# A graph layer on one Trainium2 core: comparison nodes moved to PSUM, edge statistics in groups of four banks, one spill store placed earlier

## The chip, the cores and the metric

The kernel runs on one core of a Trainium2 chip. The metric is the device time in microseconds (us) of that core; lower is better. Five engines work side by side, each with its own queue of instructions: TensorE (PE in the profile, its weight loads PEld), VectorE (DVE), ScalarE (ACT), GpSimd (POOL) and SyncE (SP). Transfers are issued by SP, ACT and POOL and carried out by 16 DMA engines.

## The reference

```python
def _mlp(h, W, b, gamma, beta):
    h = relu(h @ W + b)
    mu = mean(h, axis=0); var = mean(square(h - mu), axis=0)
    return gamma * (h - mu) * rsqrt(var + EPS) + beta
node_feat = _mlp(x, W_node, ...)                 # x: 12500 x 96
edge_feat = _mlp(edge_attr, W_edge, ...)         # 412500 x 4 -> 96
message   = _mlp(concat([x[row], x[col], edge_feat]), W_msg, ...)
agg       = segment_sum(message, col, 12500)
out       = layernorm(x + agg + node_feat)
```

Here `row` is the edge's source and `col` its target. The edges are sorted by target. Each of the three networks normalizes over all of its rows, so the statistics over all 412,500 edges have to be complete before a message can be made.

## The kernel before, in words

**Units.** Edges are worked on in tiles of 128, four tiles to a *group* of 512 (`GT`, `GE`), four groups to a *block* (`BG`). There are 806 groups and 202 blocks. Because the edges are sorted, a group's targets lie in a window of 31 nodes (`WN`), and the four windows of a block start 16 nodes apart (`WS`).

**Tables.** The source part of the message is a table lookup: `table` (L140) multiplies all nodes by a third of the message weights and writes `p_tab` and `q_tab` to memory. Rows of `p_tab` are fetched for every edge by `gather` (L158): one indirect DMA on POOL (L162) for each tile of 128 edges, 3223 in all. The first 48 of them take raw rows of `x` instead, before the table exists.

**Gathering ahead.** The first 26 blocks are gathered while the earlier stages run: `blocks` (L167) is a generator. Each `next(store)` issues 16 gathers on POOL into one of two `stage` buffers, and then a store of the block to a `spill` area in memory on SP's queue (L173). The order of SP and POOL is written out by hand here, so the places of the calls of `next(store)` (L182, L335, L336, L344, L349) are the places of stores in SP's queue, among the other transfers. Blocks 0 and 1 go with the first table, 2 to 5 with the second, 6 to 8 with the node stage (at its steps 0, 4 and 10), the other 17 with the edge stage. After them come the first 25 groups (100 gathers) of a ring of 25 group buffers, `pg` (L353).

**Node stage.** `nodes` (L241): 25 products of 512 nodes (L248), relu on ACT (L249), statistics on DVE (L250), normalization in place (L256, L257), then 98 products that transpose and center (L262), evacuated on DVE (L266) and stored as `y0_d` by SP (L269). SP's queue has `places` (L221) ahead of that.

**Edge stage.** `edge_norm` (L273) computes the edge network for its statistics alone. 606 products of 128 x 512 (L290: three for each block, on packed rows) are each written into one PSUM bank of a two-bank buffer `pr`, four buffers. After two products ACT takes both through relu into SBUF (`r`, L294, four buffers) and DVE runs one `bn_stats` for each (L296). The inputs `ea` are loaded by SP in chunks of eight blocks, 24 products each (L284), into two buffers. SP's queue holds these loads and the spill stores in one order: a load that waits for a buffer keeps the store behind it back, and a store that waits for its gathers keeps the load behind it back.

**Message stage.** `fast` (L365 on) works through `steps`, one for each group, in an order written out by hand for all five engines (L499). The blocks gathered on the fly ("late", 176) and the spilled ones ("early", 26, read back by L408) are mixed, about seven late to one early. For a group: `linear` (L443) makes four products z (128 x 96) in one of two PSUM buffers; `message` (L451) adds the gathered rows, `hs` = z + `pg` (L463, DVE), and every second group ACT writes relu of `hs` into `h` (L465). `sums` (L471) multiplies each tile of `h` by itself (L480), which yields both the sums by target and the Gram matrix for the statistics. For a block: `edges` (L433) makes four products into the four banks of one `pr` buffer; `prepare` turns them into the next block's `left` operand, relu on ACT (L440) and a comparison on DVE (L441); `add` takes the sums of the block out of PSUM (L493, L494). At the first group of a block, DVE also writes the rows that say which edge belongs to which node of its window (L457): `h` = (`rel` == `iota`), 128 x 496 elements. `rel` (the target's place in the block) and `iota` (the nodes' numbers, 4 x 31) both lie in SBUF.

DVE's order around a block's start is: `hs` of the last group of the block before, L457, `hs` of group 0, of group 1, of group 2, L441, L493 twice, L494. PE's order is: z of group 0, sums, z of group 1, sums, the four products of `edges`, z of group 2, sums, z of group 3, sums. A ring buffer becomes free when its group's `hs` is done; then POOL issues the four gathers of the group 25 places ahead (L528). For an early block no ring buffer is freed.

**Finish.** L704 to L734: the normalized sums are added to `y0`, the layer norm is applied and the result stored.

Of the kernel before, what the change touches and what calls it, by code (L numbers as in the profile page):

```python
# [11 lines left out]
F32 = mybir.dt.float32  # L12
I32 = mybir.dt.int32
AF = mybir.ActivationFunctionType
OP = mybir.AluOpType
AX = mybir.AxisListType
ET = mybir.EngineType
PSUM = bass.MemoryType.PSUM
DRAM = bass.MemoryType.DRAM

N, C, E, ED = 12500, 96, 412500, 4
EPS = 1e-5
P = 128
# [3 lines left out]
GT, GE, BG = 4, 512, 4  # L27
NT = -(-E // P)
NG = -(-NT // GT)
NBL = -(-NG // BG)  # L30
NTP, NGP = NBL * BG * GT, NBL * BG
EP = NGP * GE
EK = ED + 1
Q = 32
NS = 3
# [12 lines left out]
WN, WS, WM = 31, 16, 7  # L48
# [6 lines left out]
SKEW = 6  # L55
HB, RB = 2, 3
CL, CE = 2, 2
J = 8


# [12 lines left out]
def gnn(ctx, tc, t):  # L73
    nc = tc.nc
# [26 lines left out]
    iota = const.tile([P, BG, WN], F32, name="iota")  # L101
# [4 lines left out]
    wide = const.tile([P, P], F32, name="wide")  # L106
# [70 lines left out]
    store = blocks()  # L177
# [12 lines left out]
    for i in range(NS):  # L190
        k, n = Q * i, C - Q * i
# [81 lines left out]
    def edge_norm():  # L273

        with tc.tile_pool(name="es", bufs=2) as work, tc.tile_pool(name="es1", bufs=1) as one, \
                tc.tile_pool(name="es_ps", bufs=4, space=PSUM) as ps:
            stats = one.tile([P, NS, NBL, 6], F32, name="estats")
            for b in range(NBL):
                if b % J == 0:
                    yield  # L280
                    ea = work.tile([P, J, GE], F32, name="ea")
                    n = min(J, NBL - b)
                    for i in range(NS):
                        nc.sync.dma_start(ea[Q * i:Q * i + 2 * EK, :n, :],  # L284
                                          t["ea"][EK * i:EK * (i + 2), b:b + n, :])
                for i in range(NS):
                    k = NS * b + i
                    if k % 2 == 0:
                        pr = ps.tile([P, 2, GE], F32, name="pr")
                    nc.tensor.matmul(pr[:, k % 2, :], wide[Q * i:Q * i + 2 * EK, :],  # L290
                                     ea[Q * i:Q * i + 2 * EK, b % J, :], start=True, stop=True)
                    if k % 2:
                        r = work.tile([P, 2, GE], F32, name="r", bufs=4)
                        nc.scalar.activation(r, pr, AF.Relu)  # L294
                        for o in (1, 0):
                            nc.vector.bn_stats(stats[:, (k - o) % NS, (k - o) // NS, :], r[:, 1 - o, :])  # L296

            part = one.tile([P, NS, 2], F32, name="part")
            square = one.tile([P, NS], F32, name="square")
            for i in range(NS):  # L300
                nc.vector.bn_aggr(part[:, i, :], stats[:, i, :, :].rearrange("p a b -> p (a b)"))
            nc.vector.tensor_mul(square, part[:, :, 0], part[:, :, 0])
            nc.vector.tensor_add(part[:, :, 1], part[:, :, 1], square)
            pick = one.tile([P, NS, C], F32, name="pick")
            nc.vector.memset(pick, 0.0)
            for i in range(NS):
                for o in range(-P * i % C - C, P, C):
                    lo, hi = max(o, 0), min(o + C, P)
                    if lo < hi:
                        to = pick[:, i, lo - o:hi - o]  # L310
                        nc.vector.tensor_add(to, to, ident[:, lo:hi])
            pm = ps.tile([C, 2], F32, name="pr")
            for i in range(NS):
                nc.tensor.matmul(pm, pick[:, i, :], part[:, i, :], start=i == 0, stop=i == NS - 1)
            aggr = one.tile([C, 2], F32, name="eaggr")
            nc.vector.tensor_scalar(aggr, pm, float(NBL * GE) / E, None, op0=OP.mult)
            sq = one.tile([C, 1], F32, name="sq")
            nc.vector.tensor_mul(sq, aggr[:, 0:1], aggr[:, 0:1])
            nc.vector.tensor_sub(sq, aggr[:, 1:2], sq)
            nc.vector.tensor_scalar(aggr[:, 1:2], sq, 0.0, None, op0=OP.max)  # L320
            a_e, c_e = norm(aggr, v["g_edge"], v["beta_edge"], "edge")
            pb = ps.tile([1, C], F32, name="pr")
            nc.tensor.matmul(pb, c_e, w_msg[:, 2, :], start=True, stop=True)
            nc.vector.tensor_add(bias, pb, b_msg)
            nc.vector.tensor_scalar(w_e, w_msg[:, 2, :], a_e, None, op0=OP.mult)

    def fast(ring):
# [3 lines left out]
        with tc.manual_schedule(engines={ET.SP, ET.Pool}):  # L331
            with tc.tile_pool(name="tab_w", bufs=1) as work, tc.tile_pool(name="tab_ps", bufs=2, space=PSUM) as ps:
                for i, _ in enumerate(table(q_tab[WM:WM + NN, :], w_msg[:, 1, :], work, ps, (nc.sync,), 8)):
                    if i in (0, 2, 5):
                        next(store)  # L335
            next(store)  # L336
            nc.sync.dma_start(q_tab[:WM, :], zero[:WM])
            for r in range(WM + NN, WT, 64):
                n = min(64, WT - r)
                nc.sync.dma_start(q_tab[r:r + n, :], zero[:n])  # L340
            places()
            for i, _ in enumerate(nodes()):
                if i in (0, 4, 10):
                    next(store)  # L344
            xpool.close()
            n = 0
            for i, _ in enumerate(edge_norm()):
                if 73 * i >= 50 + 100 * n:
                    next(store, None)  # L349
                    n += 1  # L350
            for _ in store:
                pass
            got = {g: ahead_of(g) for g in range(SPILL, SPILL + RING)}  # L353
# [11 lines left out]
        with tc.tile_pool(name="fix", bufs=1) as fix, tc.tile_pool(name="msg", bufs=2) as work, \  # L365
# [11 lines left out]
            hb = [fix.tile([P, BG, GT, P], F32, name=f"h{i}") for i in range(HB)]  # L377
            for x in hb:
                nc.vector.memset(x[:, :, :, C:C + 1], 1.0)

            eas, block, prs, zs, pas, pair = {}, {}, {}, {}, {}, [None]

# [60 lines left out]
            def linear(k):  # L443
                s, g = steps[k]
                n = min(GT, NT - g * GT)
                zs[k] = ps.tile([P, GT, C], F32, name="z")
                for i in range(n):
                    nc.tensor.matmul(zs[k][:, i, :], left[s % 2][:KR, g % BG, i * P:(i + 1) * P],  # L448
                                     rhs[:KR, s % RB, g % BG, :], start=True, stop=True)

            def message(k):  # L451
                s, g = steps[k]
                n = min(GT, NT - g * GT)
                i = g % BG
                h, z, pg = hb[s % HB], zs.pop(k), got.pop(g)
                if i == 0:
                    nc.vector.tensor_tensor(  # L457
                        h[:, :, :, C + 1:C + 1 + WN], rel[:, g:g + BG, :].unsqueeze(3).to_broadcast([P, BG, GT, WN]),
                        iota.unsqueeze(2).to_broadcast([P, BG, GT, WN]), op=OP.is_equal)
                if i % 2 == 0:  # L460
                    pair[0] = work.tile([P, 2, GT, C], F32, name="hs")
                hs = pair[0]
# [35 lines left out]
            n, ahead = len(steps), SPILL + RING  # L498
# [270 lines left out]
```

## Time and profile before

| what | value |
|---|---|
| median of three runs | 5365.72 us (5353.82 to 5367.68) |
| the profiled execution's own time | 5379.39 us |
| its span in the profile | 5377.6 us |
| granted TensorE clock, mean | 0.665 |
| tables and node stage | 0 to 304 us |
| edge stage (L284 to the last L296) | 304 to 1006 us |
| message stage (first to last L463) | 1045 to 5314 us |
| finish | 5323 to 5378 us |

The page of a profile gives, engine by engine, the busy time and its share of the span, then the costliest groups of instructions: line, engine, operation, output and inputs, shapes, how many, total busy time, mean time of one in ns, and the idle time of the engine just before them with what ended it. A timeline row gives the start, the duration, the engine and line, and in brackets the idle time before and who ended it; "remote" and "issue" mean that the profile names no instruction as the releaser. A windows row gives, for a stretch of time, each engine's busy us (and the number of instructions), then TensorE's clock, the share of the DMA engines and GB/s. Ends of matmuls are modelled: when PE's products really are complete is seen better from the start of the instruction that waits for them.

### The profile page before, as it was taken

What the parts mean: (1) busy time and instruction counts of PE and PEld (TensorE: products, weight loads), DVE (VectorE), ACT (ScalarE), POOL (GpSimd) and SP (SyncE); (2) the same over time, 40 slices, a digit from 0 to 9 for tenths busy, and PEclk for the clock granted to TensorE, in tenths of its full rate; (3) what the DMA queues carried; (4) which work ended last, traced back from release to release, by engine and by line L of the source; (5) the groups of instructions that cost most, each with busy time, mean ns of one, the idle gap of its engine ahead of it and who ended that gap; (6) DMA issues with size and microseconds to landing.
All of it is one profiled execution on the core that took longest, in us unless ns stands there. A gap on an engine that the chain in (4) does not pass through costs nothing. (4 is left out here: it accounts for less than half of the span.)

```text
span 5377.6 us, 46715 instructions
## 1 busy us (share of the span) xinstructions
PE 3364.1 (63%) x16705; PEld 2570.3 (48%) x16705; DVE 1699.3 (32%) x2622; ACT 1077.6 (20%) x1015; POOL 3106.6 (58%) x3244
## 2 busy tenths in 40 slices
PE   5566662666656666665667666656666666666668
PEld 5333330354545545544445554544455545545447
DVE  1445551622222322222222322322232222223225
ACT  0224441411111111111111111111111111111112
POOL 5454456155566656666666666666666666666661
PEclk9755555566666766667676766666766666666667
DMA  5332332111111111111111111111111111111112
GB/s 165 112 97 61 71 68 48 29 33 37 39 44 38 43 42 44 43 38 42 42 43 45 42 38 43 44 42 45 37 43 42 41 45 36 43 43 42 44 37 84
DMA packets 188578, 270.80 MB, mean 50 GB/s; under 512 B 121095, under 2 KB 121480, under 8 KB 187330
## 3 DMA queue, kind: packets, MB, share of 16 engines
q0 software_dynamic: 103136, 158.62, 12.2%
q1 hardware_dynamic: 77120, 98.40, 6.6%
q10 hardware_dynamic: 8080, 10.71, 0.7%
q8 instruction: 133, 2.18, 0.2%
q14 instruction: 109, 0.89, 0.1%
HBM read 225.90 MB, written 41.60 MB: 50 GB/s over the span
## 5 line engine op out<-in xcount | busy, mean ns | idle before, releaser
L162 POOL DMA_INDIRECT pg<-p_tab,src x2807 | 2690.8, 959 | 1767.1 <-DVE hs L463 922.8
L448 PE MATMUL z<-rhs,left 128*128 128x96 f32 x6446 | 1222.7, 339 | 878.3 <-issue 672.8
L448 PEld LDWEIGHTS z<-rhs,left 128*128 128x128 f32 x6446 | 1093.2, 249 | 1183.6 <-issue 903.1
L480 PE MATMUL pa<-h 128*97 128x128 f32 x6446 | 1246.3, 331 | 556.2 <-issue 551.6
L480 PEld LDWEIGHTS pa<-h 128*97 128x97 f32 x6446 | 1015.4, 209 | 654.7 <-issue 653.3
L463 DVE TENSOR_TENSOR hs<-z,pg 128x384 f32<-128x384 f32 x702 | 385.2, 555 | 2599.2 <-remote 1537.6
L465 ACT ACTIVATE h<-hs 128x768 f32<-128x768 f32 x402 | 338.9, 843 | 2867.6 <-DVE hs L463 1846.0
L290 PE MATMUL pr<-ea,wide 10*128 10x512 f32 x1212 | 405.4, 1074 | 285.7 <-issue 177.6
L162 POOL DMA_INDIRECT stage<-p_tab,src x368 | 351.0, 954 | 369.6 <-DMA spill<-stage 240.0
L440 ACT ACTIVATE left<-pr 96x2048 f32<-96x2048 f32 x202 | 377.2, 1867 | 643.6 <-remote 439.7
L441 DVE TENSOR_SCALAR left<-pr 31x2048 f32<-31x2048 f32 x202 | 462.9, 2291 | 108.3 <-ACT left L440 75.5
L296 DVE BATCH_NORM_STATS2 estats<-r 128x6 f32<-128x512 f32 x606 | 365.8, 678 | 326.8 <-issue 191.1
L433 PE MATMUL pr<-ea,we 6*127 6x512 f32 x1404 | 411.1, 808 | 62.6 <-issue 47.5
L290 PEld LDWEIGHTS pr<-ea,wide 10*128 10x128 f32 x1212 | 209.6, 320 | 480.2 <-issue 291.8
L294 ACT ACTIVATE r<-pr 128x1024 f32<-128x1024 f32 x303 | 297.1, 1024 | 458.0 <-remote 290.0
L433 PEld LDWEIGHTS pr<-ea,we 6*127 6x127 f32 x1404 | 117.9, 223 | 206.6 <-issue 190.6
L457 DVE TENSOR_TENSOR h<-rel,iota 128x496 f32<-128x496 f32 x202 | 134.6, 666 | 0.0
L463 DVE TENSOR_TENSOR hs<-z,pb 128x384 f32<-128x384 f32 x104 | 56.6, 554 | 233.1 <-remote 85.2
L150 PE MATMUL pt<-w_msg,xp 96*128 96x96 f32 x392 | 88.7, 421 | 60.4 <-issue 37.1
L493 DVE TENSOR_TENSOR agg<-pa,agg 97x62 f32 x404 | 90.1, 223 | 85.4 <-remote 54.8
L150 PEld LDWEIGHTS pt<-w_msg,xp 96*128 96x128 f32 x392 | 85.5, 330 | 63.4 <-issue 48.6
L494 DVE TENSOR_TENSOR gram<-pa,gram 97x388 f32<-97x388 f32 x202 | 111.4, 551 | 0.1
(107 smaller groups left out, 634.7 us busy)
## 6 DMA issues: line engine op xcount, KB each, us to landing
pg<-p_tab,src POOLq DMA_INDIRECT x2807
spill<-stage SPq DMA_DIRECT2D x26, 768.0 KB
pb<-spill SPq DMA_DIRECT2D x26, 768.0 KB
ea<-in_ea SPq DMA_DIRECT2D x75, 160.0 KB
rhs<-q_tab SPq DMA_DIRECT2D x202, 46.5 KB
ea<-in_ea SPq DMA_DIRECT2D x352, 20.0 KB
stage<-p_tab,src POOLq DMA_INDIRECT x368
q_tab<-trow SPq DMA_DIRECT2D x7, 672.0 KB
```

The lines of the kernel that those rows point to most:

```text
L150: nc.tensor.matmul(pt[:, g, :], xp[:, k:k + P], w, start=True, stop=True)
L162: nc.gpsimd.indirect_dma_start(out=pg[:, i, :], out_offset=None, in_=tab[:, :], in_offset=bass.IndirectOffsetOnAxis(ap=idx[:, k:k + 1], ax ...
L290: nc.tensor.matmul(pr[:, k % 2, :], wide[Q * i:Q * i + 2 * EK, :], ea[Q * i:Q * i + 2 * EK, b % J, :], start=True, stop=True)
L294: nc.scalar.activation(r, pr, AF.Relu)
L296: nc.vector.bn_stats(stats[:, (k - o) % NS, (k - o) // NS, :], r[:, 1 - o, :])
L433: nc.tensor.matmul(prs[s][:C + WN, i, :], we[Q * i:Q * i + EK + 1, :], block[s][Q * i:Q * i + EK + 1, :], start=True, stop=True)
L440: nc.scalar.activation(x[:C, :n, :], pr[:C, :n, :], AF.Relu)
L441: nc.vector.tensor_scalar(x[C:C + WN, :n, :], pr[C:C + WN, :n, :], 0.0, None, op0=OP.is_equal)
L448: nc.tensor.matmul(zs[k][:, i, :], left[s % 2][:KR, g % BG, i * P:(i + 1) * P], rhs[:KR, s % RB, g % BG, :], start=True, stop=True)
L463: nc.vector.tensor_add(hs[:, i % 2, :n, :], z[:, :n, :], pg[:, :n, :])
L465: nc.scalar.activation(h[:, i - 1:i + 1, :, :C], hs, AF.Relu)
L480: nc.tensor.matmul(pas[s][:, g % BG, :C + 1 + WN], h[:r, i, :C + 1], h[:r, i, :C + 1 + WN], start=i == 0, stop=i == n - 1)
```

## The change

Three edits. The nodes' numbers that the comparison at a block's start reads are copied once to the unused columns 384 to 507 of one of the two PSUM banks of z, which are now allocated by hand, and the comparison reads them there. Since reader and writer share a bank, the built program has the comparison (L466 there) wait for TensorE's z of group 0, which it did not do before; `hs` of group 0 stands behind it, as before. The edge statistics go through PSUM and ScalarE four products at a time instead of two; `pr` has two buffers of four banks instead of four of two, `r` three buffers of four instead of four of two. And one `next(store)` is added ahead of the node stage, behind `places`; the edge stage then has one block less to gather and store, the last. The number of instructions on PE, POOL and SP stays as it was; ACT has 151 fewer relus in the edge stage, and DVE one copy more.

```diff
+BANKS = 4
...
     def edge_norm():
-                tc.tile_pool(name="es_ps", bufs=4, space=PSUM) as ps:
+                tc.tile_pool(name="es_ps", bufs=2, space=PSUM) as ps:
...
                     k = NS * b + i
-                    if k % 2 == 0:
-                        pr = ps.tile([P, 2, GE], F32, name="pr")
-                    nc.tensor.matmul(pr[:, k % 2, :], wide[Q * i:Q * i + 2 * EK, :],
+                    if k % BANKS == 0:
+                        pr = ps.tile([P, BANKS, GE], F32, name="pr")
+                    nc.tensor.matmul(pr[:, k % BANKS, :], wide[Q * i:Q * i + 2 * EK, :],
                                      ea[Q * i:Q * i + 2 * EK, b % J, :], start=True, stop=True)
-                    if k % 2:
-                        r = work.tile([P, 2, GE], F32, name="r", bufs=4)
-                        nc.scalar.activation(r, pr, AF.Relu)
-                        for o in (1, 0):
-                            nc.vector.bn_stats(stats[:, (k - o) % NS, (k - o) // NS, :], r[:, 1 - o, :])
+                    if k % BANKS == BANKS - 1 or k == NS * NBL - 1:
+                        r = work.tile([P, BANKS, GE], F32, name="r", bufs=3)
+                        n = k % BANKS + 1
+                        nc.scalar.activation(r[:, :n, :], pr[:, :n, :], AF.Relu)
+                        for o in range(n):
+                            j = k - n + 1 + o
+                            nc.vector.bn_stats(stats[:, j % NS, j // NS, :], r[:, o, :])
...
             places()
+            next(store)
             for i, _ in enumerate(nodes()):
                 if i in (0, 4, 10):
                     next(store)
...
+            zb = [ps.tile([P, GE], F32, name=f"z{i}", bufs=1) for i in range(2)]
+            nodes_of = zb[0][:, GT * C:GT * C + BG * WN].rearrange("p (k w) -> p k w", w=WN)
+            nc.vector.tensor_copy(nodes_of, iota)
...
             def linear(k):
-                zs[k] = ps.tile([P, GT, C], F32, name="z")
+                zs[k] = zb[k % 2][:, :GT * C].rearrange("p (t c) -> p t c", c=C)
...
                     nc.vector.tensor_tensor(
                         h[:, :, :, C + 1:C + 1 + WN], rel[:, g:g + BG, :].unsqueeze(3).to_broadcast([P, BG, GT, WN]),
-                        iota.unsqueeze(2).to_broadcast([P, BG, GT, WN]), op=OP.is_equal)
+                        nodes_of.unsqueeze(2).to_broadcast([P, BG, GT, WN]), op=OP.is_equal)
```

## The prediction, made before the changed kernel ran

> **What bounds the kernel now.** I read the page first: busy shares, then the costliest groups.
>
> ```profile
> PE 3364.1 (63%) x16705; PEld 2570.3 (48%) x16705; DVE 1699.3 (32%) x2622; ACT 1077.6 (20%) x1015; POOL 3106.6 (58%) x3244
> ...
> L162 POOL DMA_INDIRECT pg<-p_tab,src x2807 | 2690.8, 959 | 1767.1 <-DVE hs L463 922.8
> ...
> L463 DVE TENSOR_TENSOR hs<-z,pg 128x384 f32<-128x384 f32 x702 | 385.2, 555 | 2599.2 <-remote 1537.6
> ...
> L296 DVE BATCH_NORM_STATS2 estats<-r 128x6 f32<-128x512 f32 x606 | 365.8, 678 | 326.8 <-issue 191.1
> ...
> L294 ACT ACTIVATE r<-pr 128x1024 f32<-128x1024 f32 x303 | 297.1, 1024 | 458.0 <-remote 290.0
> ...
> L457 DVE TENSOR_TENSOR h<-rel,iota 128x496 f32<-128x496 f32 x202 | 134.6, 666 | 0.0
> ```
>
> No engine is full, and PE and POOL wait for each other through `hs`. The windows view says what ends last. Here are two blocks of the message stage (the first without gathers, near the end; the second with) and two stretches of the edge stage (with and without); the columns after the length are busy us of PE, PEld, DVE, ACT, POOL, then TensorE's clock.
>
> ```profile
> 5263.63:5272.85 9.22, 8.47 (x74) 7.38 (x74) 5.84 (x9) 3.56 (x3) 0.00 (x0) 1.00 0.02 7
> 2517.40:2539.70 22.30, 12.70 (x72) 10.57 (x72) 5.94 (x10) 3.56 (x3) 14.42 (x16) 0.73 0.14 35
> ```
>
> ```profile
> 840.00:860.00 20.00, 3.70 (x8) 1.01 (x8) 2.57 (x4) 2.05 (x2) 15.13 (x16) 0.50 0.23 50
> 940.00:960.00 20.00, 20.00 (x75) 11.99 (x72) 20.00 (x35) 16.66 (x18) 0.00 (x0) 0.50 0.30 63
> ```
>
> The same block takes 9.2 us without gathers and 22.3 us with 16 of them; in the edge stage PE makes four products in 20 us under gathers and some 37 without. So PE crawls while POOL gathers, and after an uninterrupted *train* of gathers it stands almost still: the timeline of the edge stage has relus of two products 10.5 to 11.2 us apart from 802 to 913 us, against 0.9 to 1.6 us outside. Why, the trace does not name; that it holds is enough. The timeline of the block above shows how the message stage turns:
>
> ```profile
> 2514.12 0.95 POOL L162 DMA_INDIRECT pg<-p_tab,src  x1 [3.28 <-DVE hs L463]
> ...
> 2517.87 0.95 POOL L162 DMA_INDIRECT pg<-p_tab,src  x1 [0.30 <-issue]
> 2518.30 0.55 DVE L463 TENSOR_TENSOR hs<-z,pg 128x384 f32<-128x384 f32 x1
> 2518.77 0.67 DVE L457 TENSOR_TENSOR h<-rel,iota 128x496 f32<-128x496 f32 x1
> ...
> 2519.12 1.13 POOL L162 DMA_INDIRECT pg<-p_tab,src  x1 [0.30 <-issue]
> 2519.53 0.56 DVE L463 TENSOR_TENSOR hs<-z,pg 128x384 f32<-128x384 f32 x1
> 2520.56 0.95 POOL L162 DMA_INDIRECT pg<-p_tab,src  x1 [0.30 <-issue]
> ...
> 2536.80 0.56 DVE L463 TENSOR_TENSOR hs<-z,pg 128x384 f32<-128x384 f32 x1 [12.27 <-remote]
> ...
> 2537.63 0.94 POOL L162 DMA_INDIRECT pg<-p_tab,src  x1 [3.61 <-DVE hs L463]
> ```
>
> A train of 16 gathers starts 1.25 us apart (0.95 busy, 0.30 between); the ring is full, POOL stops; PE comes free, `hs` fires 2.8 us after the last gather, POOL goes on. I went through all of POOL's waits over 0.5 us in this stage: 185, 778 us in all. The 78 that follow a train of 16 gathers have a median of 3.4 us, the 52 after 17 to 20 gathers 3.7 us: the wait hardly depends on the train's length. So **the message stage is trains of gathers plus a fixed wait after each**, and a train that gets shorter shortens the stage. The row at 2519.12 is the place of the change: a gather that meets L457 takes 1.13 instead of 0.95 us.
>
> **The change part by part.**
>
> *The stretched gathers (message stage).* Gather by gather: undisturbed ones take 0.946 us, also the 268 that overlap an `hs` alone, which reads one operand from PSUM and one from SBUF. Of those that overlap L457, whose two operands lie in SBUF, 169 are longer, 1.13 to 1.50 us, together 36 us. The page agrees: (959 - 946) ns x 2807 = 36 us. The change gives L457 the operand kinds of `hs`. L457 itself should stay at 0.67 us: `hs` needs 555 ns for 384 elements and L457 666 ns for 496, which is 1 ns an element for the difference, PSUM or not. Bounds: 0 (POOL's waits grow by as much) to -36 us. 25 of the 185 waits are over 6 us; there POOL waits for an early block and a shorter train gains nothing. I take 160/185 of 36: **-31 us**.
>
> [...]
>
> *The new wait of the comparison.* L457 ran while DVE was idle before z of group 0 arrived; now it waits for that z, and `hs` of group 0 stands behind it, some 0.6 us later (in the fence L457 starts 0.76 us before `hs` and is hidden). Queued behind it on DVE: `hs` of groups 0 and 1; for them wait ACT's L465, PE's z of group 2 (its PSUM buffer), and POOL. PE has room: it makes z of group 2 only after two sums, z of group 1 and `edges`. L465 is followed on ACT by L440, which waits for `edges` (PE) anyway. POOL has none where its wait ends on this very `hs`. In 147 of the 202 blocks `hs` of group 0 waits after L457, and in 55 of them it ends a wait of POOL: at most 55 x 0.6 = +33 us, at least 0. But a longer wait is time at PE's free pace, 9.2/4 = 2.3 us a group: 0.6 us is 0.26 group, of 702/185 = 3.8 groups to a wait, so 7% of 55 waits at 3.4 us, 13 us, come back. That leaves 20; I take the middle of 0 and 20: **+10 us**.
>
> *One store sooner.* Its 16 gathers (16 x 1.25 = 20 us) move on POOL's queue from the end of the edge stage into the gap at 216 to 246 us. On SP the store waits for gathers that end at 197 us, while SP's next transfer, of `y0`, is due at 241: nothing is held up. Every later spill block, and the 100 ring gathers behind the last, moves up by one place. But the gap was PE's good time:
>
> ```profile
> 214.93 0.95 POOL L162 DMA_INDIRECT stage<-p_tab,src  x1 [0.30 <-issue]
> 215.63 0.68 ACT L249 ACTIVATE agg<-pn,vec 96x512 f32<-96x512 f32 x1 [4.92 <-remote]
> ...
> 219.84 2.55 ACT L249 ACTIVATE agg<-pn,vec 96x512 f32<-96x512 f32 x4 [3.53 <-PE pn L248]
> ...
> 246.31 0.95 POOL L162 DMA_INDIRECT stage<-p_tab,src  x1 [30.43 <-DMA spill<-stage]
> ```
>
> At 216 us six of the 25 node products are left. Under gathers they come 5.6 us apart (210.03 to 215.63), so four more by 238 us, and the statistics end some 19 us later than at 223 us; everything up to the edge stage shifts with them. The edge stage has 606 products at 0.57 us (37 in 20 us is the free rate) = 345 us of its 692 us to the last relu; the other 347 us go to 17 blocks and 100 ring gathers, 23.25 trains of 16: 15 us each. One train less there, 19 us more in the node stage: **+4 us**, bounds -15 (the gap hides it) and +19 (the edge stage gives nothing back).
>
> *Four banks.* ACT: 303 x 1.02 us become 151 x 1.87 (a relu of 2048 elements, as L440) + 1.02, 26 us less. Cover: in free stretches VectorE is full (20.00 of 20), its `bn_stats` 0.593 us apart, 2.37 us for four against ACT's 1.87; under gathers PE's products end last. Neither changes. When PE's pace changes, some nine times, four products instead of two must be ready: up to 9 x 1.1 = +10 us; `r` holds 12 products instead of 8, which at best keeps VectorE busy 4 x 0.593 us longer each time: -21 us. I take **0**. The copy of `iota` (below 0.4 us) lies among memsets before the first z: 0.
>
> Sum: -31 + 10 + 4 + 0 = -17 us on the profiled 5379.4 us (span 5377.6 and 1.8 around it): 5362. That execution lies 13.7 us above the median of the runs shown, so 5349 in their terms.
>
> **Rivals.**
>
> *The waits take it up.* If `hs` comes when PE has finished a fixed amount of work, not a fixed time after the train, POOL waits longer by what it gathers faster. For: PE has no work to spare under gathers. Against: the waits' independence of the train's length. -31 becomes 0, the new wait costs nothing either: +4, about 5370.
>
> *More than the sum.* The stretch goes wholly, the new wait is free (POOL's restart falls where PE is ahead), and the early block hides: -36 + 0 - 15 = -51: 5315. For it speaks that in the 50 gather-free us after 5252 `hs` of group 0 has a microsecond of room to `hs` of group 1.
>
> *Slower: the comparison in front of `hs`.* Mechanism: L457 now starts when z of group 0 is complete, in the 147 blocks where it was hidden; 0.6 us each, at most +88 us. It decides if more than 72 of the 147 pass their 0.6 us on to POOL's restart (43 us against the -31 and +4 above, which leaves +16). With 110: 66 - 31 + 4 = +39, 5405. For it: DVE's strict order and 147 waits. Against: only 55 of these `hs` release POOL today.
>
> **How the numbers follow.** A measurement of this kernel tells about 0.3% (16 us) from no change. Forecast (0 to -40 us): 0.45, of which 0.27 beyond 0.3% and 0.18 within. Waits take it up: 0.18, within. More than the sum: 0.15. Slower: 0.22. Hence faster 0.42, same 0.36, slower 0.22. The predicted time is the forecast's, 5349. The range reaches from below the second rival (5305) into the third (5385, +20); left out are some 0.06 below and 0.14 above. It takes in the stretch's bounds (0, -36), the store's (-15, +19), and those of the four banks.
>
> **What would show it.** Right: L162's mean at 946 to 948 ns and no gather over 1 us beside the comparison; the comparison's row at about 0.67 us with idle time before it released by PE's z; L249's last relu at some 242 us; the last L296 at 1005 to 1015 us; the message stage some 20 us shorter. Wrong: stretched gathers that remain; POOL's waits on `hs` well above 778 us in sum or more than 185; an edge stage that moves by more than 20 us, which would say that pace changes and not VectorE set it.

## The result, and the profile after

The changed kernel takes **5444.06 us** (median of 4 runs, 5431.77 to 5448.6), the kernel before in the same job 5361.52 (4 runs): ratio **1.0155, 95% interval 1.0137 to 1.0173**, 82.5 us slower. I had predicted 5349 and a range of 5305 to 5385. The profiled execution of the changed kernel took 5448.6 us (span 5446.9). Line numbers of after are those of before +1 (L162 is L163), +3 at the end of the edge stage, +9 in the message stage (L463 is L472, L457 is L466).

One thing has to be known for the numbers below. The runs were made in jobs, each on one chip. In some jobs TensorE crawls beside gathers as the prediction describes, and the kernel before takes 5359 to 5394 us; in others it doesn't, and the same program takes 4167 to 4177 us. I speak of crawling and free chips; the five jobs of the experiments had five different chips, so whether this goes with the chip or with the time is not shown. Each run is compared with the kernel before in its own job only. The pair above was made on a crawling chip.

The page of after, rows that answer to those of before:

```profile
L163 POOL DMA_INDIRECT pg<-p_tab,src x2807 | 2647.9, 943 | 1860.3 <-DVE hs L472 1038.6
...
L472 DVE TENSOR_TENSOR hs<-z,pg 128x384 f32<-128x384 f32 x702 | 383.6, 553 | 1962.0 <-remote 1400.2
...
L299 DVE BATCH_NORM_STATS2 estats<-r 128x6 f32<-128x512 f32 x606 | 368.2, 679 | 379.3 <-ACT r L296 193.6
...
L296 ACT ACTIVATE r<-pr 128x2048 f32<-128x2048 f32 x152 | 278.2, 1870 | 528.9 <-remote 288.9
L466 DVE TENSOR_TENSOR h<-rel,z 128x496 f32<-128x496 f32 x202 | 135.0, 668 | 669.6 <-remote 343.1
```

The gathers do take 943 instead of 959 ns, and not one of the 2807 is over 1 us. (128 of before are; the 169 of my prediction were too many, the 36 us in all hold.) But POOL's idle time ahead of them grew from 1767 to 1860 us, by 93 us, more than the 43 us by which their busy time fell. Some 53 of the 93 are one wait, for the first `hs` behind a longer edge stage. Before, then after:

```profile
1046.17 0.95 POOL L162 DMA_INDIRECT pg<-p_tab,src  x1 [131.22 <-DVE hs L463]
```

```profile
1117.89 0.94 POOL L163 DMA_INDIRECT pg<-p_tab,src  x1 [184.64 <-DVE hs L472]
```

The other 39 or so lie in the message stage and take up what the gathers save there. The comparison, which had no idle time before it (0.0), now has 670 us. And `bn_stats` is now held up by ACT's relu, where before the releaser was "issue".

Stage by stage in the two traces, in us:

| | before | after | difference |
|---|---|---|---|
| last relu of the node stage | 223.3 | 243.3 | +20.0 |
| last `y0` copy to last `bn_stats` | 303.8 to 1005.6 | 324.0 to 1071.2 | +45.4 |
| last `bn_stats` to first L441/L450 | 35.3 | 40.9 | +5.6 |
| first to last `hs` | 4268.7 | 4265.9 | -2.8 |
| span | 5377.6 | 5446.9 | +69.3 |

The rest to 82.5 us is that the profiled execution of before lay 17.9 us above its median and that of after 4.5. The table asks two questions: why the edge stage became longer, and where the message stage's 36 us of shorter gathers went.

The edge stage first: the windows view of after, one stretch under gathers and one free of them (columns as in the prediction).

```profile
840.00:860.00 20.00, 2.32 (x7) 1.18 (x8) 2.34 (x4) 1.88 (x1) 15.12 (x17) 0.50 0.19 39
1000.00:1020.00 20.00, 19.03 (x58) 7.23 (x56) 16.20 (x27) 13.37 (x8) 0.00 (x0) 0.50 0.17 25
```

Under gathers nothing changed: four `bn_stats` in 20 us, as before. The free stretch did: 27 instead of 35, and VectorE is no longer full (16.2 us of 20). The timeline of that stretch:

```profile
1000.20 3.65 ACT L296 ACTIVATE r<-pr 128x2048 f32<-128x2048 f32 x2 [2.14 <-PE pr L291]
1002.11 4.84 DVE L299 BATCH_NORM_STATS2 estats<-r 128x6 f32<-128x512 f32 x8 [0.95 <-ACT r L296]
...
1002.13 5.55 PE L291 MATMUL pr<-ea,wide 10*128 10x512 f32 x16 [0.24 <-ACT r L296]
...
1005.99 3.65 ACT L296 ACTIVATE r<-pr 128x2048 f32<-128x2048 f32 x2 [2.14 <-PE pr L291]
```

Two relus run back to back (3.65 us), then ACT waits 2.14 us for PE, and so on: eight products in 5.79 us, 0.72 each, against 0.57 before. The single records say why. A product is two passes (1212 records of L291 for 606 products), and PE runs the passes of three products (one block's, on three groups of rows) side by side: three start at 996.335, .341 and .348 us and take 1.22 us each, the next three start about 0.85 to 1.0 us later. A group of four cuts the second triple: product 4 lies in one buffer, 5 and 6 in the other. So the triple waits until the other buffer's relu has ended, and the first buffer's relu waits until the triple, which holds its last product, has run. ACT and PE wait for each other in turn.

The +5.6 us behind it has a row too. The three `bn_aggr` of 5.5 us each lie on VectorE, the first of them in before ahead of the last two `bn_stats`, while VectorE waited for the last pair; in after all three come last. Before:

```profile
999.46 5.62 DVE L301 BATCH_NORM_AGGREGATE part<-estats 128x2 f32<-128x1212 f32 x1
1005.01 1.22 DVE L296 BATCH_NORM_STATS2 estats<-r 128x6 f32<-128x512 f32 x2
1006.14 11.09 DVE L301 BATCH_NORM_AGGREGATE part<-estats 128x2 f32<-128x1212 f32 x2
```

After:

```profile
1071.78 16.57 DVE L304 BATCH_NORM_AGGREGATE part<-estats 128x2 f32<-128x1212 f32 x3
```

Then the message stage, in the timeline of after at the end of a train:

```profile
2710.24 0.95 POOL L163 DMA_INDIRECT pg<-p_tab,src  x1 [0.30 <-issue]
...
2714.42 0.67 DVE L466 TENSOR_TENSOR h<-rel,z 128x496 f32<-128x496 f32 x1 [12.41 <-PE pa L489]
2715.01 1.01 DVE L472 TENSOR_TENSOR hs<-z,pg 128x384 f32<-128x384 f32 x2
2715.83 0.94 POOL L163 DMA_INDIRECT pg<-p_tab,src  x1 [4.64 <-DVE hs L472]
```

VectorE idles 12.41 us, makes the comparison first, then `hs` of groups 0 and 1, and only then POOL goes on. POOL's waits over 0.5 us on `hs` are 185 as before, but 817 us in sum against 778.

### The profile page after: what moved, and what is told of

It is laid out like the page before. It is cut to its first block, busy times and chain, and to the rows that moved or that the text cites. A ratio compares the mean times of both kernels' runs of the same rounds, so it can differ in the third digit from the quotient of the medians.

```text
span 5446.9 us, 46571 instructions
## 1 busy us (share of the span) xinstructions
PE 3364.7 (62%) x16705; PEld 2520.0 (46%) x16705; DVE 1698.9 (31%) x2623; ACT 1054.2 (19%) x864; POOL 3063.7 (56%) x3244
## 5 line engine op out<-in xcount | busy, mean ns | idle before, releaser
L163 POOL DMA_INDIRECT pg<-p_tab,src x2807 | 2647.9, 943 | 1860.3 <-DVE hs L472 1038.6
L457 PE MATMUL z<-rhs,left 128*128 128x96 f32 x6446 | 1243.9, 334 | 1035.1 <-issue 672.9
L457 PEld LDWEIGHTS z<-rhs,left 128*128 128x128 f32 x6446 | 1103.8, 246 | 1330.7 <-issue 869.7
L489 PE MATMUL pa<-h 128*97 128x128 f32 x6446 | 1213.6, 330 | 433.5 <-issue 431.2
L472 DVE TENSOR_TENSOR hs<-z,pg 128x384 f32<-128x384 f32 x702 | 383.6, 553 | 1962.0 <-remote 1400.2
L291 PE MATMUL pr<-ea,wide 10*128 10x512 f32 x1212 | 447.1, 1098 | 296.9 <-issue 150.1
L163 POOL DMA_INDIRECT stage<-p_tab,src x368 | 351.1, 954 | 390.0 <-DMA spill<-stage 256.3
L450 DVE TENSOR_SCALAR left<-pr 31x2048 f32<-31x2048 f32 x202 | 462.9, 2292 | 182.0 <-ACT left L449 109.2
L291 PEld LDWEIGHTS pr<-ea,wide 10*128 10x128 f32 x1212 | 166.7, 315 | 576.0 <-issue 312.1
L296 ACT ACTIVATE r<-pr 128x2048 f32<-128x2048 f32 x152 | 278.2, 1870 | 528.9 <-remote 288.9
L466 DVE TENSOR_TENSOR h<-rel,z 128x496 f32<-128x496 f32 x202 | 135.0, 668 | 669.6 <-remote 343.1
L472 DVE TENSOR_TENSOR hs<-z,pb 128x384 f32<-128x384 f32 x104 | 57.5, 553 | 134.3 <-PE z L457 93.0
```

The source lines that it names most:

```text
L163: nc.gpsimd.indirect_dma_start(out=pg[:, i, :], out_offset=None, in_=tab[:, :], in_offset=bass.IndirectOffsetOnAxis(ap=idx[:, k:k + 1], ax ...
L291: nc.tensor.matmul(pr[:, k % BANKS, :], wide[Q * i:Q * i + 2 * EK, :], ea[Q * i:Q * i + 2 * EK, b % J, :], start=True, stop=True)
L296: nc.scalar.activation(r[:, :n, :], pr[:, :n, :], AF.Relu)
L450: nc.vector.tensor_scalar(x[C:C + WN, :n, :], pr[C:C + WN, :n, :], 0.0, None, op0=OP.is_equal)
L472: nc.vector.tensor_add(hs[:, i % 2, :n, :], z[:, :n, :], pg[:, :n, :])
L489: nc.tensor.matmul(pas[s][:, g % BG, :C + 1 + WN], h[:r, i, :C + 1], h[:r, i, :C + 1 + WN], start=i == 0, stop=i == n - 1)
```

## The experiments

**1. Each edit alone.** Theory A: the four banks set the edge stage's pace, and the waits take up what the gathers save. First job, a free chip (before 4166.95 us). The edits as diffs, each on the kernel before:

```diff
# e1_psum: the comparison's nodes in the bank of even groups' z
+            zb = [ps.tile([P, GE], F32, name=f"z{i}", bufs=1) for i in range(2)]
+            nodes_of = zb[0][:, GT * C:GT * C + BG * WN].rearrange("p (k w) -> p k w", w=WN)
+            nc.vector.tensor_copy(nodes_of, iota)
...
-                zs[k] = ps.tile([P, GT, C], F32, name="z")
+                zs[k] = zb[k % 2][:, :GT * C].rearrange("p (t c) -> p t c", c=C)
...
-                        iota.unsqueeze(2).to_broadcast([P, BG, GT, WN]), op=OP.is_equal)
+                        nodes_of.unsqueeze(2).to_broadcast([P, BG, GT, WN]), op=OP.is_equal)
# e2_banks: edge_norm as in the changed kernel
+BANKS = 4
# e3_store
             places()
+            next(store)
# f_zb1: as e1_psum, but in the bank of odd groups' z
+            nodes_of = zb[1][:, GT * C:GT * C + BG * WN].rearrange("p (k w) -> p k w", w=WN)
```

> The kernel before with the comparison's nodes in the bank of z of even groups, and nothing else. Theory A (the waits take it up): the stretched gathers vanish (mean of the message stage's gathers 959 to 943 ns), POOL's waits grow by as much, and the time is within 10 us of before. Rival B (the gain of 31 us is there and the changed kernel loses it to what the other two edits do to the message stage): 20 to 36 us faster than before.

> The kernel before with edge products in groups of four banks, two such buffers, and nothing else. Theory A (the pace of the edge stage outside the trains of gathers is now that of PE and ScalarE passing two buffers to and fro, 0.73 us a product instead of 0.57): 40 to 60 us slower, the edge stage longer by as much, relus of 1.87 us in pairs with about 2.1 us idle before each pair. Rival B (the four banks cost nothing; the edge stage of the changed kernel is longer because its trains begin at another moment): within 10 us of before.

> The kernel before with one store more ahead of the node stage, and nothing else. Theory A (the node stage ends 20 us later, and the edge stage, with a block of gathers less, ends its free stretches at the old pace and so gives 15 us of it back): 0 to 8 us slower. Rival B (nothing is given back, as in the changed kernel, whose last ring gather came 18 us later): 15 to 25 us slower.

> The comparison's nodes in PSUM as in the first of these runs, but in the bank of z of odd groups: the products in it are those of the block before, long done, so the comparison keeps a PSUM operand and loses its wait for z of group 0. Theory A1 (the new wait gave the gain back): 20 to 36 us faster than before. Rival A2 (POOL's wait after a train ends when PE has done a fixed amount of work, whatever the comparison waits for): the same time as the first of these runs within 8 us.

| run | median, us | against before | ratio, 95% |
|---|---|---|---|
| e1_psum | 4129.35 | -37.6 | 0.9911 (0.9896 to 0.9926) |
| e2_banks | 4219.73 | +52.8 | 1.0121 (1.0106 to 1.0137) |
| e3_store | 4152.63 | -14.3 | 0.9970 (0.9960 to 0.9980) |
| f_zb1 | 4132.58 | -34.4 | 0.9917 (0.9903 to 0.9930) |

On this chip it was rival B that held for the comparison (37.6 us, just over its 36), and theory A for the banks. The store missed both of its theories, which had it slower. f_zb1 lies within both of its ranges and decides nothing. The windows view of e1_psum in the edge stage, and its gathers on the page:

```profile
400.00:420.00 20.00, 20.00 (x72) 13.90 (x70) 20.00 (x35) 17.31 (x17) 14.85 (x17) 0.50 0.60 99
```

```profile
L162 POOL DMA_INDIRECT pg<-p_tab,src x2807 | 2648.4, 944 | 856.2 <-issue 785.1
```

PE makes 35 products in 20 us *beside* 17 gathers, where the crawling chip has four. So POOL sets the end: nearly all of its idle time is "issue", the 0.3 us between two gathers, and after 570 us no gap between two gathers is more than 0.5 us longer than that, up to the last gather. What POOL saves is saved: 36 us of stretched gathers. The store fills a gap of 16 us at 176 us (a wait for an earlier store) and gains 10 to 14. The banks lengthen the edge stage from 367 (e1_psum) to 438 us. Spill stores that stand behind the later loads on SP then hold POOL up (63 us of waits for them against 20 in e1_psum, of which 18 and 16.5 come at 176 us, ahead of the edge stage), and at the end POOL stands before the full ring, in the timeline of e2_banks:

```profile
716.27 0.94 POOL L163 DMA_INDIRECT pg<-p_tab,src  x1 [0.30 <-issue]
732.63 0.94 POOL L163 DMA_INDIRECT pg<-p_tab,src  x1 [15.42 <-DVE hs L466]
```

My premise for f_zb1 was wrong, and its page showed it. The product of the next group is issued ahead of a group's message, so the odd bank has just been given z of group 1, and the comparison waits longer than with the even bank. Its row in e1_psum, then in f_zb1:

```profile
L461 DVE TENSOR_TENSOR h<-rel,z 128x496 f32<-128x496 f32 x202 | 134.9, 668 | 91.5 <-PE z L452 91.5
```

```profile
L461 DVE TENSOR_TENSOR h<-rel,z 128x496 f32<-128x496 f32 x202 | 135.6, 671 | 590.3 <-PE z L452 590.3
```

So f_zb1 doesn't take the wait away; where POOL sets the end, neither wait costs anything.

**2. The crawl again: combination, and what in the banks costs.** Second job, a crawling chip (before 5394.20 us): the changed kernel, the changed kernel with two-bank groups, and two forms of the edge stage alone.

```diff
# d13_two_banks: the changed kernel, its edge_norm as before
-BANKS = 4
-                tc.tile_pool(name="es_ps", bufs=2, space=PSUM) as ps:
+                tc.tile_pool(name="es_ps", bufs=4, space=PSUM) as ps:
...
# b3_three_banks: edge_norm of the changed kernel alone, on the kernel before
+BANKS = 3
# p2_two_buffers: the kernel before
-                tc.tile_pool(name="es_ps", bufs=4, space=PSUM) as ps:
+                tc.tile_pool(name="es_ps", bufs=2, space=PSUM) as ps:
```

> The changed kernel itself, beside the kernel before on this chip. If before takes 5361 us as in the first pair, again some 80 us slower. If it takes some 4167 us as in the four single edits, two theories: A (GpSimd never waits in that mode except for the ring to be emptied, so a store sooner only makes it wait longer for the first hs, which the edge stage delays by 70 us): -37 for the comparison, +53 for the banks, 0 for the store, together 10 to 20 us slower. B (the three edits add up): -37 + 53 - 14 = 2, within 6 us of before.

> The changed kernel with the two-bank groups of before in the edge stage (so the comparison's nodes in PSUM, and the store sooner). Where before takes 4167 us: theory A (both are time of GpSimd's, which never waits) 45 to 55 us faster; rival B (the sooner store's gain lies in gathers beside the comparison too, so the two overlap) 34 to 40 us faster. Where before takes 5361 us: theory A (the waits take the gathers' gain up, the node stage's 20 us are partly given back by the edge stage's old pace) 0 to 20 us slower; rival B 20 us faster or more.

> The kernel before with edge products in groups of three banks, two such buffers (six banks), instead of two banks and four buffers. TensorE runs the products of one block of edges in threes, beside each other. Theory A (a group of four cuts such a triple in two, and that, with two buffers, made 0.73 us a product): groups of three keep the triples whole, 0.57 to 0.60 us a product, time within 12 us of before. Rival B (only the number of buffers counts, two being too few for PE and ScalarE to overlap): 0.68 to 0.75 us a product, 35 to 60 us slower.

> The kernel before with groups of two banks, but two PSUM buffers instead of four (four banks in all). Theory A (triples cut in two and two buffers: PE waits for ScalarE's release within a triple): 0.70 us a product or more, 35 us slower or more. Rival B (the length of the relu, 1.87 us against 1.02, is what stretches the passing to and fro; with short relus two buffers do): 0.57 to 0.62 us a product, within 12 us of before.

| run | median, us | against before | ratio, 95% | free pace, us a product |
|---|---|---|---|---|
| after_again | 5487.16 | +93.0 | 1.0181 (1.0164 to 1.0197) | 0.76 |
| d13_two_banks | 5429.15 | +34.9 | 1.0068 (1.0052 to 1.0084) | 0.66 |
| b3_three_banks | 5413.48 | +19.3 | 1.0039 (1.0025 to 1.0053) | 0.65 |
| p2_two_buffers | 5510.88 | +116.7 | 1.0225 (1.0205 to 1.0245) | 0.87 |

(Free pace: `bn_stats` counted from 6 us after a train's end to the next train's start; the kernel before has 0.65 by the same count, the changed one 0.76.) The banks cost 58 us, after_again less d13_two_banks. d13_two_banks is slower than both of its theories allowed (0 to 20 us slower, or 20 faster). b3_three_banks lies between its two theories in time; its pace has to be set against the 0.65 that this count gives before, not the 0.57 of my expectation, which came from one window. Three banks with two buffers have fewer banks in use than either kernel (six) and the pace of before, because the triples stay whole; two buffers of two banks, whose triples are cut as well and whose relu is the short one, are slowest. That refutes "the length of the relu" and "two buffers are too few", and leaves, of the explanations I had, the cut triple with too few buffers to cover it. In b3_three_banks ACT is released by PE after half a microsecond:

```profile
1001.10 1.45 ACT L296 ACTIVATE r<-pr 128x1536 f32<-128x1536 f32 x1 [0.43 <-PE pr L291]
...
1002.91 1.45 ACT L296 ACTIVATE r<-pr 128x1536 f32<-128x1536 f32 x1 [0.36 <-PE pr L291]
```

Three products in 1.8 us here. In p2_two_buffers two take 1.7, as ACT's relu, shorter by 0.43 us, waits longer:

```profile
838.36 1.02 ACT L294 ACTIVATE r<-pr 128x1024 f32<-128x1024 f32 x1 [0.53 <-PE pr L290]
...
840.05 1.02 ACT L294 ACTIVATE r<-pr 128x1024 f32<-128x1024 f32 x1 [0.67 <-PE pr L290]
```

The 19 us of b3_three_banks are not pace: its trains cost PE 28 us for 32 gathers against 26, and 8 to 10 for 16 against 6, about 20 us in all.

This job also holds a comparison of message stages. b3_three_banks and p2_two_buffers have the one of before: 4280.7 and 4278.4 us from the first to the last `hs`. after_again and d13_two_banks have the changed one: 4304.2 and 4318.4, so 24 to 40 us longer, although their gathers in it are 23 to 44 us shorter in sum; POOL's waits on `hs` grew by 48 to 83 us. As its edge stage is as long as that of before, most of the 34.9 us of d13_two_banks must lie there.

**3. Does the comparison's wait eat the gain?** A form without it: the comparison behind `hs` of group 1, reading the odd bank, whose z that `hs` has just used.

```diff
# g_later, on f_zb1 ("best" is g_later with the store of e3_store)
-                if i == 0:
-                    nc.vector.tensor_tensor(
-                        h[:, :, :, C + 1:C + 1 + WN], rel[:, g:g + BG, :].unsqueeze(3).to_broadcast([P, BG, GT, WN]),
-                        nodes_of.unsqueeze(2).to_broadcast([P, BG, GT, WN]), op=OP.is_equal)
...
                 nc.vector.tensor_add(hs[:, i % 2, :n, :], z[:, :n, :], pg[:, :n, :])
+                if i == 1:
+                    nc.vector.tensor_tensor(
+                        h[:, :, :, C + 1:C + 1 + WN], rel[:, g - 1:g - 1 + BG, :].unsqueeze(3).to_broadcast([P, BG, GT, WN]),
+                        nodes_of.unsqueeze(2).to_broadcast([P, BG, GT, WN]), op=OP.is_equal)
```

> The comparison's nodes in the bank of z of even groups, nothing else; once more, to have it where TensorE crawls beside gathers (before at 5360 to 5400 us). There theory A (the comparison's new wait for z of group 0 pushes every hs back) and theory B (GpSimd waits for a TensorE that crawls, so what the gathers save is waited for) both say 5 to 35 us slower, and against both stands my forecast of 20 us faster. Where before takes 4167 us again, 37 us faster as the first time.

> The nodes in the bank of z of odd groups, so that the comparison waits for no new product, beside the run with the even bank. With before at 5360 to 5400 us: theory A (the new wait ate the gain) 20 to 36 us faster than before; theory B (a crawling TensorE sets the restart of GpSimd whatever the comparison waits for) as the even bank within 10 us. With before at 4167 us: 34 us faster, as the first time, by both.

> As the odd bank, and the comparison stands behind hs of group 1 instead of ahead of hs of group 0, where its 0.67 us delays neither. With before at 5360 to 5400 us: theory A (0.67 us ahead of hs of group 0 is the price) 30 to 45 us faster than before; theory B (TensorE sets it) within 10 us of the two other forms, as the block's first sums need the comparison anyway. With before at 4167 us: by both as the odd bank, 34 us faster within 6.

> One store sooner and nothing else, once more. With before at 5360 to 5400 us: theory A (a train of 16 gathers costs TensorE 6 us, one of 32 costs 26, so what counts is how trains join; in the node stage the longer train costs up to 20 us, in the edge stage 8 come back) between 5 us faster and 15 slower; rival B (the node stage's 20 us pass on whole) 15 to 25 us slower. With before at 4167 us, 14 us faster as the first time.

The third job fell on a free chip (before 4177.41 us) and so told no theories apart: 4139.60, 4138.98, 4137.49 and 4167.33 us, ratios 0.9905 (0.9890 to 0.9920), 0.9906 (0.9891 to 0.9921), 0.9905 (0.9889 to 0.9920) and 0.9975 (0.9964 to 0.9986). It repeats the first. The fourth was on a crawling chip again (before 5358.97 us):

> The changed kernel. With before at 5360 to 5400 us: 75 to 95 us slower, as twice before. With before at 4167 to 4177 us: theory A (the edge stage, 70 us longer by the banks, keeps GpSimd waiting for the first hs, and a store sooner only lengthens that wait) 10 to 20 us slower; rival B (the parts add up, -37 + 53 - 12) within 6 us of +4.

> The changed kernel with two-bank groups. With before at 5360 to 5400 us: 25 to 45 us slower, as before. With before at 4167 to 4177 us: theory A (both edits save time of GpSimd, which never waits) 45 to 55 us faster, rival B (they overlap) 34 to 40 us faster.

> The kernel before with the nodes in the bank of z of odd groups, the comparison behind hs of group 1, and the store sooner; two-bank groups as before. With before at 5360 to 5400 us: theory A (the new wait ate the gathers' gain) 15 to 36 us faster than before, that is 45 us or more below the even bank with the store; theory B (a crawling TensorE sets GpSimd's restart) within 12 us of the even bank with the store, 20 to 45 us slower than before. With before at 4167 to 4177 us: 45 to 55 us faster than before, as the even bank with the store.

| run | median, us | against before | ratio, 95% | first to last `hs` | POOL's waits over 0.5 us |
|---|---|---|---|---|---|
| after_third | 5437.94 | +79.0 | 1.0139 (1.0118 to 1.0159) | 4269.1 | 821 |
| d13_again | 5383.45 | +24.5 | 1.0042 (1.0026 to 1.0057) | 4269.5 | 819 |
| best | 5352.33 | -6.6 | 0.9984 (0.9970 to 0.9999) | 4235.4 | 790 |

The banks cost 54.5 us again. With the later comparison the kernel is 31 us faster than with the even bank, and its message stage 34 us shorter, at the same 943 to 944 ns a gather. In the timeline of best POOL goes on before the comparison has begun, and on its page the comparison has no idle time:

```profile
2636.70 0.94 POOL L162 DMA_INDIRECT pg<-p_tab,src  x1 [0.31 <-issue]
...
2640.61 1.02 DVE L464 TENSOR_TENSOR hs<-z,pg 128x384 f32<-128x384 f32 x2 [11.43 <-remote]
2641.44 0.94 POOL L162 DMA_INDIRECT pg<-p_tab,src  x1 [3.80 <-DVE hs L464]
2641.55 0.66 DVE L466 TENSOR_TENSOR h<-rel,z 128x496 f32<-128x496 f32 x1
```

```profile
L466 DVE TENSOR_TENSOR h<-rel,z 128x496 f32<-128x496 f32 x202 | 133.3, 660 | 0.0
```

So theory A holds for direction: the comparison in the even bank, in front of `hs` of group 0, had eaten what best has back, 31 us where theory B allowed 12. best changes the bank and the place at once, so which of the two counts is left open. For size theory A fell short: I expected 15 to 36 us below before and 45 or more below d13_again, and 6.6 and 31 were measured. Part of the gap is the store: the node stage of best ended at 241.9 us, that of d13_again at 231.7, and its first `hs` came 12 us later.

**4. Whole gain, and the sum on a free chip.** The last job was to show the two parts without the store on a crawling chip, but fell on a free one (before 4176.03 us).

> Odd bank, comparison in its old place ahead of hs of group 0, no store. With before at 5340 to 5400 us: theory A (the wait for z of group 0, not the 0.67 us in front of hs, ate the gain; as in the kernel before the comparison runs while VectorE is idle) 20 to 36 us faster; rival B (the place) 0 to 10 us faster. With before at 4167 to 4177 us, 34 to 38 us faster, as twice before.

> Odd bank, comparison behind hs of group 1, no store. With before at 5340 to 5400 us, by both theories 20 to 36 us faster, as the message stage of the run with the store was 33 us shorter; if it is within 10 us of before, the store was what gained. With before at 4167 to 4177 us, 38 us faster, as before.

> Odd bank, later comparison, the store sooner. With before at 5340 to 5400 us: 0 to 12 us faster, as before. With before at 4167 to 4177 us: theory A (GpSimd never waits, so both edits save its time) 45 to 55 us faster, rival B (they overlap) 34 to 40 us faster.

4137.02, 4137.86 and **4127.98 us**; ratios 0.9902 (0.9886 to 0.9919), 0.9907 (0.9891 to 0.9924) and 0.9881 (0.9864 to 0.9897). The store adds 10 us to the comparison's 38: both are time of POOL's, and they add up. "best" is the version to keep: two-bank groups, nodes in PSUM, later comparison, the store sooner; it is below the kernel before on both kinds of chip, clearly on a free one, on a crawling one by 6.6 us, an interval that ends just short of no change. Where the changed kernel was measured beside it, best is 85.6 us below that.

**Open.** Whether the changed kernel loses or gains on a free chip was not measured (its parts sum to -37.6 + 52.8 - 14.3 = +1). Whether the wait for z or the place ahead of `hs` costs the 31 us was not separated on a crawling chip. Nor was g_later run there; traces give best a message stage 33 us shorter than before's, times only 6.6 us in all, so part of the former may be that the execution profiled of before was 17.9 us above its median. The same shows in d13_again: 24.5 us above before in time, its trace's span (5372.8) 4.8 us below that of before. So of the message stage only comparisons within a job are firm: the 31 us between d13_again and best, and the 24 to 40 us of the second job. Why the second job's wait cost more than the fourth's is not shown.

## Why the prediction was wrong, step by step

- **Four banks, predicted 0 (bounds -21 to +10): measured +54.5 and +58.** This is the step that failed most. Its words were "in free stretches VectorE is full ... Neither changes". I compared ACT's relu with `bn_stats` as rates, 1.87 against 2.37 us, and asked only whether ACT is fast enough. With half as many buffers and groups that cut PE's triples, PE and ACT overlap less, and VectorE, which had been busy for all of a free stretch, was busy for 81% of it. The prediction's own test ("an edge stage that moves by more than 20 us ... would say that pace changes and not VectorE set it") caught it. To it belong 5.6 us of a `bn_aggr` that lost its cover.
- **The new wait, predicted +10 (bounds 0 to +33): +31 in time, +34 in the trace, against the later comparison; more in the second job.** The mechanism was right; the step that failed is "a longer wait is time at PE's free pace ... 13 us, come back", and taking the middle of what was left. In d13_again 51 of the comparisons that run straight into `hs` end a wait of POOL: 51 x 0.67 = 34 us. Nothing came back. In the second job the message stage was 24 to 40 us longer although its gathers were shorter, so the bound of 33 did not hold there, unless PE's pace took up what the gathers saved as well (the first rival); no run separates the two. There 69 such comparisons in after_again and 67 in d13_two_banks end a wait of POOL, some 45 us.
- **Stretched gathers, -31: all 36 us gone wherever the nodes lie in PSUM**, and worth 34 to 40 us on free chips, where POOL sets the end. With iota in SBUF 128 (before), 111 (e2_banks) and 111 (e3_store) gathers take over 1 us, together 36 us each time; in after, e1_psum, f_zb1, g_later and best none does. (In the trace of before the stretched ones take 1.05 to 1.50 us, not 1.13 to 1.50, and 424 rather than 268 gathers overlap an `hs` alone, at the same 0.946 us.) In that trace 230 gathers overlap the comparison, all 128 long ones among them; in the trace of after 155 do, and none takes over 0.96 us. By what a comparison with both operands in SBUF lengthens a gather, no run here shows.
- **One store sooner, +4 (bounds -15 to +19): not measured alone on a crawling chip, -14 and -10 on free ones.** Kernels with it and two-bank groups had their first `hs` at 1039.4, 1043.5 and 1051.4 us (d13_again, d13_two_banks, best) against 1045.3 before: no clear net. The node stage ended at 243.3 us, predicted 242, but in other executions with the same order between 226.9 and 243.6. The price "15 us each" for a train was wrong in kind: in the trace of before PE loses 6 us to a train of 16 gathers, 26 to one of 32 and 120 to one of 116 (the train and 6 us after it, less its products at the free pace of 0.65), as the crawl sets in 10 to 15 us after a train begins. (The 0.57 us a product of that sum was the rate of one window; over all free stretches it is 0.65.) A train taken out of the edge stage only makes the last one longer (132 gathers, 134 us in after and 137 in d13_two_banks), so the edge stage gave little back: in d13_two_banks it is as long as before (690.0 against 690.6 us).
- **Copy of `iota`, 0: 0.29 us**, right.
- **The rivals.** The slower one (0.22, 5405 us) named the comparison in front of `hs`, at 110 blocks x 0.6 = 66 us; the 31 us of the fourth job are half of that, and the second job's traces allow more. None had the four banks at a cost: I gave that edit one answer without a rival, and some 55 of the 82.5 us lie there. In the table of stages the rest is the node stage's +20 and a message stage in which the gathers' gain and the wait's loss cancel to -2.8, so "the waits take it up" (0.18) described that stage of that pair best, by the mechanism of the other rival.

The comparison waits although its columns (384 to 507) are not those of z (0 to 383), and the wait goes with the bank: in the first job its row has no idle time with `iota` in SBUF (e3_store, 0.0), 91.5 us put down to z with the nodes in the even bank (e1_psum) and 590.3 in the odd one (f_zb1); in after it has 670. Why, no run shows. The wait need not lie on the critical spot, as best shows with 0.0.

## What to carry to other kernels

Count a chain of producer, evacuation and consumer by its cycle (who must have ended before whom can start), not by comparing rates: two buffers of four banks left VectorE's sum as it was (366 us before, 368 after), shortened ScalarE's (297 to 278) and lost part of the overlap (0.65 to 0.76 us a product), while two buffers of three banks, which hold whole sets of the products that run side by side, kept it (0.65). The operand moved into a bank that TensorE writes brought TensorE's wait with it here (0.0 us of idle time before the comparison, then 670); put such an instruction where the wait has already been served, behind the one that releases the bottleneck (0.0 again in best). And give each edit a rival of its own, above all the one costed at nothing.

## What the runs showed of the hardware that I had not expected

The same program takes 5359 to 5394 us on some chips and 4167 to 4177 on others, with gathers of 0.94 to 0.96 us in the mean, 0.3 us between them, on both. The difference is TensorE beside gathers: 4 products in 20 us against 35. Its mean granted clock over the whole run was 0.66 and 0.74 to 0.75, but in the two stretches compared here it was 0.50 on both, so the clock does not explain them. On a crawling chip the crawl begins 10 to 15 us after a train does (relus then 4.2 to 5.6 us apart in the node stage of before, against 0.86 ahead of it), and ends with it. PE's weight loads and passes then start in steps: from 2705 to 2713 us in the trace of after each comes 0.7 or 1.4 us behind the one before. Five jobs and the first pair were split three to three; the three with the changed kernel were the crawling ones, but the kernel before crawled in them too. What makes TensorE crawl, no run here shows.
